# Summing the last MLP chunk's activations in three pieces of 128 tokens, one ahead of each tile

## The chip, the cores and the metric

The kernel runs on one core of one Trainium2 chip. The metric is device time in microseconds (us) for one execution. Before the change it is 2811.47 us, the median of three runs that lie between 2810.86 and 2814.71 us. All data are 32-bit floats.

## What is computed

The reference is one transformer block on a 48 x 48 grid of tokens with 768 channels, followed by a spectral layer on the same grid. Cut to what matters here:

```
x   = x + attention(layernorm(x)) @ proj_w + proj_b
xn2 = layernorm(x)
h   = gelu(xn2 @ mlp_w1 + mlp_b1)          # 2304 x 3072
x   = x + (h @ mlp_w2 + mlp_b2)            # 2304 x 768
x   = x + irfft2(soft-shrunk two-layer mix of rfft2(x))
```

The change lies at the end of the second product of the MLP, `h @ mlp_w2`, and just ahead of the spectral layer.

## The kernel before

**Staging.** The attention comes first, then the MLP, then the spectral layer. The result `x` stays in SBUF all the time, as 18 tiles of 128 tokens by 768 channels (`main`, also called `x1`). The MLP walks over three groups of 768 tokens (`p`), and within each over 12 chunks of 256 hidden features (`n`). One chunk makes its activations `h` (2 blocks of 128 features by 768 tokens) in the generator `hidden` and adds their share of the output in `added`, in three calls `i` = 0, 1, 2. Call `i` handles two tiles of 128 tokens at once, one from each half of the group's 768 tokens. "Tile" below means such a call.

**Seven products instead of eight.** Both matrix products are split into 2 x 2 blocks and computed with seven block products (a scheme of Strassen's kind). That needs sums of blocks beforehand. For the second product, `left` (lines 160 to 164) makes them from the activations on VectorE: four operations on 128 x 384 elements. With a11, a12, a21, a22 the four blocks of `h`, line 161 writes s1 = a21 + a22, line 162 writes s2 = s1 - a11, line 163 writes s4 = a12 - s2, and line 164 overwrites a21 with s3 = a11 - a21. Both inputs of each of them lie in SBUF. Line 162 waits for 161 by a semaphore, and 163 for 162; 164 waits for nothing.

**The seven products of a tile**, in `added` (lines 1403 to 1413), in their order on TensorE:

```
nc.tensor.matmul(bank[0], a11, b11, start=True, stop=True)   # p0: needs no sum
product(1, s2, t2, True, acc[i])     # p1: needs line 162
product(2, s3, t3, True, x22)        # p2: needs line 164
product(3, s1, t1, True, x22)        # p3
product(0, a12, b21, False, x11)     # p4
product(2, a22, t4, False, x21)      # p5
product(3, s4, b22, False, x12)      # p6
```

Each is followed by one VectorE operation that reads its PSUM bank and adds it to a tile in SBUF (line 1407 for p0, line 1401 for the others). In the last chunk of a group three more additions end the tile: line 1415 on VectorE (`x21 += acc`), lines 1416 and 1417 on GpSimd (called POOL in the profile; `x12 += acc`, `x22 += acc`). All three have both inputs in SBUF.

**Order of the work.** In this part of the kernel the order on every engine is the order in which the program is written (`manual_schedule`), and every engine takes its instructions strictly in that order. Within a group, the additions of chunk n - 1 are put between the stages of `hidden` of chunk n, so that TensorE has matrix products (line 1338) while `left` runs. After the last chunk (n = 11) there is no next chunk. In groups 0 and 1, transposes (`turned`) stand ahead of each of the three calls of `added`. In the last group (p = 2) nothing stands there: the three tiles follow directly on `left`. After them `rows_forward` (line 1419) begins the spectral layer with the products `zp` of line 1431.

**The rest of the chain.** The `zp` products are copied to SBUF (`zt`), stored to DRAM by the SP queue, and loaded back in another order as `zi`. Everything after that depends on them.

Of the kernel before, what the change touches and what calls it, by code (L numbers as in the profile page):

```python
# [19 lines left out]
P = 128  # L20
HW = 48
T = HW * HW
# [7 lines left out]
TB = 768  # L30
G = 384
# [15 lines left out]
def block_then_afno(  # L47
# [27 lines left out]
    nc = tc.nc  # L75
# [15 lines left out]
    def col(i):  # L91
        return vec[:, i : i + 1]
# [67 lines left out]
    def left(eng, a11, a12, a21, a22, s):  # L160
        eng.tensor_tensor(s[0], a21, a22, ALU.add)
        eng.tensor_tensor(s[1], s[0], a11, ALU.subtract)  # L162
        eng.tensor_tensor(s[2], a12, s[1], ALU.subtract)
        eng.tensor_tensor(a21, a11, a21, ALU.subtract)  # L164
# [16 lines left out]
    def parts_of_tokens(xt, xs, at=slice(None)):  # L181

        blocks = [xt[:, ds(3 * i, 3), ts(j, G)] for i, j in ((0, 0), (1, 0), (0, 1), (1, 1))]
        return [a[:, :, at] for a in (*blocks, *(xs[:, i] for i in range(3)))]
# [10 lines left out]
    with ExitStack() as flag_scope:  # L195
# [12 lines left out]
        with ExitStack() as att:  # L208
# [491 lines left out]
            with tc.manual_schedule(engines={mybir.EngineType.PE, mybir.EngineType.SP}):  # L700
# [161 lines left out]
                with tc.manual_schedule(  # L862
                    engines={mybir.EngineType.Activation, mybir.EngineType.DVE}
                ):
                    for pr in range(NC):
                        for c in range(T // G):
# [19 lines left out]
                            work = between(pr, c, acc)  # L886
# [166 lines left out]
        with tc.If(safe < 1):  # L1053
            with ExitStack() as att:
# [27 lines left out]
                for pr in range(NC):  # L1082
# [39 lines left out]
                    for sg in range(T // SG):  # L1122
# [20 lines left out]
                        for i in range(2):  # L1143
                            hp = psum.tile([P, G], F32, name="g_hp", tag="m")
                            for r in range(8):
                                h = sg * 16 + i * 8 + r
# [104 lines left out]
        with tc.tile_pool(name="ps_turn", bufs=4, space=PSUM) as psum_turn, tc.tile_pool(  # L1251
# [3 lines left out]
            for u in range(EARLY, PAIRS):  # L1255
# [5 lines left out]
                n = u - EARLY  # L1261
# [29 lines left out]
    with ExitStack() as mlp:  # L1291
# [10 lines left out]
        n_f = FF // FCH  # L1302
# [4 lines left out]
        def weights(p, n):  # L1307

            w = wpool.tile([P, NC, FCH], F32, name="w1")
            nc.sync.dma_start(  # L1310
                out=w, in_=mlp_w1[:, ts(n, FCH)].rearrange("(c p) f -> p c f", p=P)
            )
            ws = wpool.tile([P, 3, 3, P], F32, name="w1s")
            a11, a12, a21, a22 = (w[:, ds(3 * j, 3), ts(i, P)] for i in range(2) for j in range(2))
            left(nc.gpsimd, a11, a12, a21, a22, [ws[:, i] for i in range(3)])
            v = wpool.tile([P, 2, C], F32, name="w2")
            nc.sync.dma_start(
                out=v, in_=mlp_w2[ts(n, FCH), :].rearrange("(j p) c -> p j c", p=P)
            )
            vs = wpool.tile([P, 3, CH], F32, name="w2s")  # L1320
            right(
                nc.gpsimd, v[:, 0, :CH], v[:, 0, CH:], v[:, 1, :CH], v[:, 1, CH:],
                [vs[:, i] for i in range(3)],
            )
            ready_w[p, n] = a11, a12, a21, a22, ws, v, vs

        def hidden(p, n):

            a11, a12, a21, a22, ws, v, vs = ready_w.pop((p, n))
            h = hpool.tile([P, 2, TB], F32, name="hT")  # L1330
            hs = hpool.tile([P, 3, G], F32, name="hs", bufs=1)
            kept[p, n] = h, hs, v, vs

            bank = [psum.tile([P, G], F32, name=f"h{i}") for i in range(4)]

            def product(i, a, b, start):
                for c in range(3):
                    nc.tensor.matmul(  # L1338
                        bank[i], a[:, c, :], b[:, c, :],
                        start=(start and c == 0), stop=(c == 2), skip_group_check=not start,  # L1340
                    )

            def gelu(i, k, src):
                nc.scalar.activation(  # L1344
                    h[:, i, ts(k, G)], src, AF.Gelu, bias=col(V_B1 + 2 * n + i)
                )

            def summed(src, other, name, bufs=2):
                t = upool.tile([P, G], F32, name=name, bufs=bufs)
                nc.vector.tensor_tensor(t, src, other, ALU.add)  # L1350
                return t

            b11, b21, t3, b22, t1, t2, t4 = parts_of_tokens(xt, xs)
            s1, s2, s4 = (ws[:, i] for i in range(3))
            product(0, a11, b11, True)
            m1 = upool.tile([P, G], F32, name="m1")
            nc.scalar.copy(m1, bank[0])
            product(1, s2, t2, True)
            u = summed(bank[1], m1, "u")
            yield  # L1360
            product(2, a21, t3, True)
            u7 = summed(bank[2], u, "u7")
            product(3, s1, t1, True)
            gelu(1, 1, summed(bank[3], u7, "c", 3))
            yield
            product(0, a12, b21, False)
            gelu(0, 0, bank[0])
            product(2, a22, t4, False)
            gelu(1, 0, summed(bank[2], u, "c", 3))
            product(3, s4, b22, False)  # L1370
            gelu(0, 1, summed(bank[3], u, "c", 3))
            yield
            left(
                nc.vector, h[:, 0, :G], h[:, 1, :G], h[:, 0, G:], h[:, 1, G:],
                [hs[:, i] for i in range(3)],
            )
            yield

        acc = {}

        def added(p, n, i):

            h, hs, v, vs = kept[p, n]
            bank = [psum.tile([P, CH], F32, name=f"o{k}") for k in range(4)]
            if n == 0:
                acc[i] = upool.tile([P, CH], F32, name=f"acc{i}", bufs=1)
            a11, a12, s3, a22 = (
                h[:, f, ds(k * G + i * P, P)] for f, k in ((0, 0), (1, 0), (0, 1), (1, 1))
            )
            s1, s2, s4 = (hs[:, k, ts(i, P)] for k in range(3))  # L1390
            b11, t3, b21, b22 = (v[:, f, ts(k, CH)] for f in range(2) for k in range(2))
            t1, t2, t4 = (vs[:, k] for k in range(3))
            t = 2 * (p * 3) + i
            x11, x12, x21, x22 = (
                x1[:, t + 3 * j, ts(k, CH)] for j in range(2) for k in range(2)
            )

            def product(k, a, b, start, *into):
                nc.tensor.matmul(bank[k], a, b, start=start, stop=True, skip_group_check=not start)  # L1399
                for dst in into:  # L1400
                    nc.vector.tensor_tensor(dst, bank[k], dst, ALU.add)  # L1401

            nc.tensor.matmul(bank[0], a11, b11, start=True, stop=True)  # L1403
            if n == 0:
                nc.vector.tensor_copy(acc[i], bank[0])
            else:
                nc.vector.tensor_tensor(acc[i], bank[0], acc[i], ALU.add)
            product(1, s2, t2, True, acc[i])
            product(2, s3, t3, True, x22)
            product(3, s1, t1, True, x22)  # L1410
            product(0, a12, b21, False, x11)
            product(2, a22, t4, False, x21)
            product(3, s4, b22, False, x12)
            if n == n_f - 1:
                nc.vector.tensor_tensor(x21, x21, acc[i], ALU.add)
                nc.gpsimd.tensor_tensor(x12, x12, acc[i], ALU.add)
                nc.gpsimd.tensor_tensor(x22, x22, acc[i], ALU.add)
# [61 lines left out]
        def turned(piece):  # L1479

            for i in range(4 * piece, 4 * piece + 4):
                j, c = divmod(i, NC)
                tp = psum.tile([P, G], F32, name="tp2", tag=f"h{i % 4}")
                for k in range(3):
                    nc.tensor.transpose(tp[:, ts(k, P)], hats[3 * j + k][:, ts(c, P)], ident)  # L1485
                nc.scalar.activation(
                    xt[:, c, ts(j, G)], tp, AF.Identity, bias=col(V_LN2B + c), scale=col(V_LN2G + c)
                )
# [6 lines left out]
        for p in range(T // TB):  # L1495
            for n in range(n_f):
                if (p, n) == (0, 2):
                    nc.sync.dma_start(out=b2, in_=mlp_b2[0, :].partition_broadcast(P))
                    nc.sync.dma_start(out=rows_dft, in_=c_rows)
                work = hidden(p, n)  # L1500
                for i in range(3):
                    next(work)
                    if n:
                        added(p, n - 1, i)
                next(work)
                if n < n_f - 1 and (p == 0 or n):
                    weights(p, n + 1)
                if p < 2 and 3 <= n < 9:
                    measured(p + 1, n - 3)
                if p < 2 and n > 8:  # L1510
                    for i in range(2 * (n - 9), 2 * (n - 8)):
                        normalised(p + 1, i)
            for i in range(3):
                if p < 2:
                    turned(i)
                added(p, n_f - 1, i)
            if p < 2:
                sums_of_tokens(xt, xs)
                for n in range(2):
                    weights(p + 1, n)  # L1520
            rows_forward(p)
# [392 lines left out]
```

## Time and profile before

One execution was profiled. Its own time is 2813.01 us; the span from its first to its last instruction is 2811.2 us, so 1.8 us lie around the span.

| | before |
|---|---|
| median of 3 runs | 2811.47 us (2810.86 to 2814.71) |
| profiled execution | 2813.01 us, span 2811.2 us, mean granted TensorE clock 0.998 |
| TensorE matmuls (PE) | 2781.4 us busy, 99% of the span |
| TensorE weight loads (PEld) | 1715.4 us, 61% |
| VectorE (DVE) | 1700.5 us, 60% |
| ScalarE (ACT) | 916.2 us, 33% |
| GpSimd (POOL) | 662.7 us, 24% |
| three tiles of the last chunk, p0 of the first to first `zp` | 2545.21 to 2560.66 us in the span |

How to read the views that follow. A row of the timeline has the start of an instruction in us from the span's start, how long it took in us, engine, line, operation, what it writes and reads, and, in square brackets, how long the engine sat idle before it and what ended that. "x2" merges two instructions (every 32-bit product is two matmul records). In the view by groups, a row has the busy time in us and the mean ns of one instruction after the bar. In the view of windows, a row has a stretch, its length, and per engine the busy time; PEclk is the share of the TensorE clock that was granted.

### The profile page before, as it was taken

Reading aid. Unit: us, or ns where it says so; the run is one execution under the profiler, and the core shown is the slowest. Engines: PE = TensorE matmul, PEld = TensorE weight load, DVE = VectorE, ACT = ScalarE, POOL = GpSimd, SP = SyncE. Lnnn points to the kernel's source line nnn. Section 1 sums busy time; section 2 is a strip of 40 time slices with the busy share of each in tenths; the row PEclk is TensorE's granted clock in tenths of the full one; section 3 lists DMA queues with packets and bytes.
Section 4 is the critical chain, followed back from the end, with each engine's and each line's share of the span. In section 5 each row is a group of like instructions: output and inputs, shape, how many; then the busy total and the mean of one; then the engine's idle time right before and its main releaser. Section 6 shows DMA issues by size and latency. Waiting matters only on the chain. (4 is left out here: it accounts for less than half of the span.)

```text
span 2811.2 us, 40985 instructions
## 1 busy us (share of the span) xinstructions
PE 2781.4 (99%) x15765; PEld 1715.4 (61%) x15765; DVE 1700.5 (60%) x2505; ACT 916.2 (33%) x1456; POOL 662.7 (24%) x658
## 2 busy tenths in 40 slices
PE   8999999999999999999999999999999999999998
PEld 5555656666556566665555555555555555556887
DVE  4434246767676767676756566665666566566666
ACT  1101136656566666665501101121101201102332
POOL 2405110000000000000064332352232522322433
PEclk9999999999999999999999999999999999999999
DMA  5435376273663737546242112131121212123254
GB/s 177 162 107 168 99 157 120 50 137 63 106 127 65 132 63 124 99 77 102 90 156 79 58 61 67 45 102 57 45 67 62 96 45 68 45 65 113 63 161 146
DMA packets 216848, 269.08 MB, mean 96 GB/s; under 512 B 24600, under 2 KB 195472, under 8 KB 215108
## 3 DMA queue, kind: packets, MB, share of 16 engines
q1 hardware_dynamic: 215350, 265.25, 38.0%
q8 instruction: 127, 2.08, 0.3%
q10 hardware_dynamic: 1230, 0.92, 0.1%
q14 instruction: 77, 0.63, 0.1%
q0 software_dynamic: 64, 0.20, 0.0%
HBM read 150.25 MB, written 52.32 MB: 72 GB/s over the span
## 5 line engine op out<-in xcount | busy, mean ns | idle before, releaser
L736 ACT ACTIVATE main<-sp 128x768 f32<-128x768 f32 x648 | 516.1, 811 | 34.7 <-PE sp L726 19.3
L880 DVE TENSOR_TENSOR pairs<-pairs,main 128x1536 f32<-128x1536 f32 x252 | 443.0, 1758 | 27.2 <-DVE pairs L880 0.9
L726 PE MATMUL sp<-terms,select 64*128 64x384 f32 x1296 | 412.0, 629 | 0.0
L1401 DVE TENSOR_TENSOR main<-o,main 128x384 f32<-128x384 f32 x540 | 299.3, 557 | 43.1 <-PE o L1399 0.5
L1338 PE MATMUL h<-shared,w 128*128 128x384 f32 x864 | 296.6, 486 | 0.7 <-POOL w2s L167 0.7
L717 PE MATMUL sp<-shared 64*128 64x384 f32 x1296 | 265.2, 485 | 1.6 <-ACT row_hi L241 1.0
L717 PE MATMUL sp<-qT,kT 64*128 64x384 f32 x1296 | 264.1, 484 | 0.0
L1338 PEld LDWEIGHTS h<-shared,w 128*128 128x128 f32 x864 | 163.9, 190 | 116.2 <-POOL w2s L167 1.3
L782 POOL TENSOR_TENSOR inverse<-inverse,rden 24x32 f32<-24x32 f32 x36 | 14.9, 414 | 924.9 <-DVE sums L781 924.9
L1338 PE MATMUL h<-shared,w1s 128*128 128x384 f32 x648 | 226.7, 486 | 0.0
L749 PE MATMUL op<-main,shared 128*64 128x384 f32 x1296 | 217.4, 488 | 0.0
L749 PE MATMUL op<-main,v 128*64 128x384 f32 x1296 | 216.4, 488 | 0.0
L1344 ACT ACTIVATE hT<-c,vec 128x384 f32<-128x384 f32 x108 | 66.4, 615 | 457.6 <-DVE c L1350 457.5
L880 DVE TENSOR_TENSOR pairs<-main 128x1536 f32<-128x1536 f32 x36 | 63.3, 1758 | 245.8 <-ACT main L736 245.8
L1350 DVE TENSOR_TENSOR c<-h,u 128x384 f32<-128x384 f32 x108 | 60.2, 557 | 218.5 <-PE h L1338 218.5
L726 PEld LDWEIGHTS sp<-terms,select 64*128 64x128 f32 x1296 | 125.3, 186 | 83.7
L1399 PE MATMUL o<-w2s,hs 128*128 128x384 f32 x432 | 175.0, 487 | 1.2 <-DVE hs L162 1.2
L1399 PE MATMUL o<-w,hT 128*128 128x384 f32 x432 | 175.1, 487 | 0.8 <-DVE hT L164 0.5
L1338 PEld LDWEIGHTS h<-shared,w1s 128*128 128x128 f32 x648 | 123.1, 190 | 85.8
L167 POOL TENSOR_TENSOR w2s<-w 128x384 f32<-128x384 f32 x36 | 36.0, 999 | 576.8 <-DMA w<-in_mlp_w_dram 429.4
L749 PEld LDWEIGHTS op<-main,v 128*64 128x64 f32 x1296 | 96.8, 137 | 92.7 <-issue 67.7
L749 PEld LDWEIGHTS op<-main,shared 128*64 128x64 f32 x1296 | 96.4, 137 | 89.4 <-issue 64.4
(222 smaller groups left out, 4176.9 us busy)
## 6 DMA issues: line engine op xcount, KB each, us to landing
w<-in_mlp_w_dram SPq DMA_DIRECT2D x72, 768.0 KB
terms<-col_parts SPq DMA_DIRECT2D x432, 72.0 KB
terms<-row_hi SPq DMA_DIRECT2D x216, 72.0 KB
terms<-row_lo SPq DMA_DIRECT2D x216, 72.0 KB
main<-in_qkv_w_dram SPq DMA_DIRECT2D x36, 384.0 KB
z<-zt SPq DMA_DIRECT2D x48, 192.0 KB
x<-in_x_blocks_dram SPq DMA_DIRECT2D x18, 384.0 KB
q_d<-o SPq DMA_DIRECT2D x36, 192.0 KB
```

The costliest lines, as they stand in the source:

```text
L167: eng.tensor_tensor(t[0], b12, b11, ALU.subtract)
L717: nc.tensor.matmul(sp[:, j, :G], kT[at, ts(kt, P)], qT[at, ts(c, G)], start=first, stop=not first,)
L726: nc.tensor.matmul(sp[:, j, :G], select[at, a % 2], ready[pr, c][at, a // 2, b], start=first, stop=not first,)
L736: nc.scalar.activation(p, sp[:, :, :G], AF.Exp, scale=HD**-0.5)
L749: nc.tensor.matmul(op[ts(j, 64)], v[:, kt, ts(j, 64)], exps[:, kt, j, :], start=(kt == 0), stop=(kt == NT - 1),)
L782: nc.gpsimd.tensor_tensor(inverse[:ND], inverse[:ND], rden, ALU.add)
L880: nc.vector.tensor_tensor(pairs, so_far, exps[:, ds(kt - 1, 2)], ALU.add)
L1338: nc.tensor.matmul(bank[i], a[:, c, :], b[:, c, :], start=(start and c == 0), stop=(c == 2), skip_group_check=not start,)
L1344: nc.scalar.activation(h[:, i, ts(k, G)], src, AF.Gelu, bias=col(V_B1 + 2 * n + i))
L1350: nc.vector.tensor_tensor(t, src, other, ALU.add)
L1399: nc.tensor.matmul(bank[k], a, b, start=start, stop=True, skip_group_check=not start)
L1401: nc.vector.tensor_tensor(dst, bank[k], dst, ALU.add)
```

## The change

Only in the last chunk of the last group, `left` is no longer made in one piece of 384 columns but in three pieces of 128 columns (one tile's tokens each). The first piece stands where the whole stood; the second and the third stand ahead of `added` of tile 1 and tile 2. In all other chunks the order and the sizes are as before.

```diff
@@ hidden
             yield
-            left(
-                nc.vector, h[:, 0, :G], h[:, 1, :G], h[:, 0, G:], h[:, 1, G:],
-                [hs[:, i] for i in range(3)],
-            )
-            yield
+            pieces = [slice(0, G)]
+            if (p, n) == (T // TB - 1, n_f - 1):
+                pieces = [slice(i * P, i * P + P) for i in range(3)]
+            for at in pieces:
+                left(
+                    nc.vector, h[:, 0, :G][:, at], h[:, 1, :G][:, at],
+                    h[:, 0, G:][:, at], h[:, 1, G:][:, at], [hs[:, i, at] for i in range(3)],
+                )
+                yield
@@ block_then_afno, after the loop over chunks
             for i in range(3):
                 if p < 2:
                     turned(i)
+                elif i:
+                    next(work)
                 added(p, n_f - 1, i)
```

On VectorE, four instructions on 128 x 384 become twelve on 128 x 128: four ahead of tile 0's additions, four between tile 0's line 1415 and tile 1's line 1407, and four at the same place ahead of tile 2. The order on TensorE, ScalarE, GpSimd and in the DMA queues stays as it was. On TensorE, p1 of tiles 1 and 2 now waits for VectorE (line 162 of its piece), and so does p2 (line 164 of its piece).

## Prediction

> **What bounds the kernel now.** I read the page first: TensorE's matmuls fill the span, VectorE has a third of it free.
>
> ```profile
> PE 2781.4 (99%) x15765; PEld 1715.4 (61%) x15765; DVE 1700.5 (60%) x2505; ACT 916.2 (33%) x1456; POOL 662.7 (24%) x658
> ```
>
> So a change gains only where TensorE sits idle. The list of waits in the stretch 2540 to 2562 us shows TensorE waiting for `left` once: 1.2 us for line 162 and 0.2 us for line 164. Then the timeline of the last chunk's three tiles (all engines), where I followed p0 to p6 of tile 0 and the end of its VectorE and GpSimd work:
>
> ```profile
> 2545.21 0.81 PE L1403 MATMUL o<-w,hT 128*128 128x384 f32 x2
> 2545.89 0.55 DVE L161 TENSOR_TENSOR hs<-hT 128x384 f32<-128x384 f32 x1
> 2546.47 0.56 DVE L162 TENSOR_TENSOR hs<-hs,hT 128x384 f32<-128x384 f32 x1
> ...
> 2547.17 0.88 PE L1399 MATMUL o<-w2s,hs 128*128 128x384 f32 x2 [1.15 <-DVE hs L162]
> ...
> 2548.23 0.88 PE L1399 MATMUL o<-w,hT 128*128 128x384 f32 x2 [0.18 <-DVE hT L164]
> ...
> 2550.89 0.81 PE L1399 MATMUL o<-w,hs 128*128 128x384 f32 x2
> ...
> 2552.21 0.55 DVE L1415 TENSOR_TENSOR main<-main,acc 128x384 f32<-128x384 f32 x1
> 2552.37 1.24 POOL L1416 TENSOR_TENSOR main<-main,acc 128x384 f32<-128x384 f32 x1 [26.26 <-DVE main L1401]
> ...
> 2553.57 0.99 POOL L1417 TENSOR_TENSOR main<-main,acc 128x384 f32<-128x384 f32 x1
> ```
>
> The reader is to see three things. p1 starts at 2547.17, 0.14 us after line 162 ended (2546.47 + 0.56); p2 starts at 2548.23, 0.14 us after line 164 ended. Undisturbed products follow each other every 0.645 us (2548.95, 2549.60, 2550.24, 2550.89). And VectorE ends a tile late: line 1415 starts 1.32 us after p6 started, when TensorE is already past p0 and due to start p1 of the next tile.
>
> **What is gained: tile 0.** From p0 at 2545.21, p3 was due 3 x 0.645 later, at 2547.145; it started at 2548.95. So `left` costs 1.80 us today. In the new kernel its first piece has 128 columns. No row has that width on two SBUF inputs; by form, a VectorE operation on two tensors takes 254 ns for 96 columns (line 1630), 351 for 192 (line 1656) and 554 for 384 (line 1656). Between the first two, 128 columns take about 0.285 us. The shortest VectorE row I found (209 ns, line 1462) and the 0.555 us of the full width are the bounds; I take 0.285, which lies between its two nearest widths. Line 161 starts at 2545.89 as before, since VectorE is busy with the tile ahead until then; 162 starts 0.03 after 161 ends (as in the rows) and ends at 2546.49; p1 starts at 2546.63, where it was due at 2545.855: 0.78 lost, and 0.07 more because the product after a stall took 0.72 instead of 0.645 (2548.23 to 2548.95). Line 164 ends at 2547.01 (it starts 0.08 before 163's end, as in the rows), ahead of p2's turn at 2547.345. Loss 0.85 instead of 1.80: **0.95 us gained**.
>
> **What is added: tiles 1 and 2.** Here there is no wait before; the sums are long made. Now VectorE makes piece 1 after tile 0's line 1415, and p1 of tile 1 waits for it. Call X the start of the previous tile's p6 (2550.89 above). p1 is due at X + 1.29. Line 1415 starts at X + 1.32, and the instruction behind it started 0.46 later in the old order (2552.67), so line 161 can start at X + 1.78, end of 162 at X + 2.38, p1 at X + 2.52: 1.23 + 0.07 = 1.30 us lost, even if nothing disturbs VectorE. On VectorE, all of the tile's seven additions are queued behind the piece, but they wait for TensorE's products anyway.
>
> Something does disturb it. GpSimd runs lines 1416 and 1417 of the tile before from X + 1.48 to X + 3.67, and they have two SBUF inputs as the four lines of `left` have. What that means is seen in the first chunk of the MLP (timeline from 1560 us), where GpSimd's sums of weights meet `left`:
>
> ```profile
> 1561.59 0.56 DVE L163 TENSOR_TENSOR hs<-hT,hs 128x384 f32<-128x384 f32 x1
> 1561.66 1.34 POOL L161 TENSOR_TENSOR w1s<-w 128x384 f32<-128x384 f32 x1 [5.23 <-DMA w<-in_mlp_w_dram]
> 1562.07 1.35 DVE L164 TENSOR_TENSOR hT<-hT 128x384 f32<-128x384 f32 x1
> ```
>
> Line 164 took 1.35 us instead of its usual 0.55, and GpSimd's 1.34 instead of 1.00. They took turns: GpSimd had to let 163 end, then 164 had to let GpSimd end (at 1563.00) and ended 0.42 us after it. Line 1416's own 1.24 us beside line 1415 are the same thing. So in tile 1: 1416 has waited since X + 1.48 and goes as soon as 1415 is through, ends at X + 2.72 (as today, 2553.61), and line 161 ends 0.15 after it (0.42 less 0.27 for 256 columns fewer), at X + 2.87. Line 1417, at its place since X + 2.68, goes next, before line 162, which must first see 161's semaphore at X + 2.90; 1417 needs 1.00 and ends at X + 3.72. Line 162 ends 0.15 later, at X + 3.87, and **p1 starts at X + 4.01**. Lost: 4.01 - 1.29 + 0.07 = 2.79 us. Lines 163 and 164 then have the way free; 164 ends at X + 4.39, p2 could start at X + 4.53 and is due at X + 4.73, no further stall. Tile 2 repeats this: 5.58 us in all. If VectorE went first instead, I get 161 undisturbed but 162 behind 1416 and 163 behind 1417, p2 late, and about 2.5 us a tile: the turn hardly matters.
>
> Nothing covers it: TensorE takes its products in order and `zp` (line 1431) follows 0.74 us behind the last p6. No DMA and no other engine's order is moved; all after `zp` depends on it and shifts along. Sum so far: 5.58 - 0.95 = **+4.63 us**.
>
> **The clock.** TensorE idles from the end of p0 (X + 0.645 + 0.81) to X + 4.01: 2.55 us, twice. In the trace, changes of the granted clock fall on a grid of 3.41 us. I asked the windows view for the stretches ahead of the two drops; the second, near the end:
>
> ```profile
> 2792.70:2796.11 3.41, 1.36 (x18) 0.97 (x16) 1.24 (x4) 0.00 (x0) 0.00 (x0) 1.00 0.68 224
> 2796.11:2799.52 3.41, 3.41 (x25) 3.15 (x23) 1.07 (x3) 0.00 (x0) 0.00 (x0) 0.50 0.68 229
> ```
>
> After a stretch with TensorE busy for 1.36 of 3.41 us (one gap of 2.05 us, waiting for `zl`) the next stretch ran at half clock. After 1.15 busy us (1464.91 on; a gap of 3.76 us) it was two stretches. After 2.50 busy us (2543.52 on, the stall of tile 0 today) the clock stayed at 1.00. A gap of 2.55 us leaves only 0.86 us of busy time if it lies within one stretch. It has at least 2.05 us in one stretch for 1.86 of the 3.41 us of possible positions, 55%; if a smaller share is enough (anything down to the 0.92 us that did no harm), up to 100%. I take 75% for each gap. A drop costs 3.41 us at half rate, all of it in products where the stretch begins behind the gap (1.7 us lost), less where up to 0.5 us of the gap lies in it (1.45): 1.6. Two drops: **+3.2 us**.
>
> The Trainium skill, on its page "TensorE: Matmul & The Clock Gate", section "Why this matters for your kernels", asks only that TensorE's idle gaps stay under about 3 us. By that rule the gaps of 2.55 us would cost no clock and the sum would stay at +4.6; this case's row with a gap of 2.05 us and half a clock behind it speaks against it, and I go by the row.
>
> **The sum.** -0.95 + 5.58 + 3.2 = +7.8 us: the profiled execution would go from 2813.01 (span 2811.2 and 1.8 around it) to 2820.8. That execution lay 1.54 above the median of the runs; from the median 2811.47, **2819.3 us**. What a measurement of this kernel can tell from no change is about 0.2%, or 5.6 us.
>
> **The rivals.**
> 1. *Lock without drops, or with one.* The position of the stretches is chance: one drop gives 4.63 + 1.6 = +6.2 (2817.7), none +4.6 (2816.1), not measurably slower. For it: no stretch with a busy time between 1.36 and 2.50 us was seen at full clock, and the 1.36 were narrower matmuls (64 columns).
> 2. *VectorE and GpSimd don't collide.* If a 128-column operation slips between GpSimd's reads, only 2 x 1.30 - 0.95 = +1.65 us remains, and gaps of 1.06 us (X + 1.455 to X + 2.52) that trip nothing: 2813.1. Against it: line 164's 1.35 us and line 1416's 1.24.
> 3. *The other side: it does what it says.* If pieces 1 and 2 were ready before p1's turn, only tile 0's gain stays: -0.95, 2810.5, not slower. It decides itself at one point: line 162 of a piece must end by X + 1.15 (p1's turn less 0.14). VectorE would have to make the piece in a hole ahead of p6's addition; but it takes its instructions in order, and line 1415, ahead of the piece, starts only at X + 1.32.
>
> **How the numbers follow.** Forecast, collision with two drops, 33%; one drop 27%; none 15%; no collision 15%; the pieces cost nothing 4%; more than any of these, 6%. The range: the low end takes in no collision, 2813.0. For the high end I take the full-width price for a 128-column operation: 0.27 more for each of lines 161 and 162, three times 0.54 = +1.6, with two drops 2820.9, and some 0.6 for the spread of the runs: 2821.5. At the cheapest price, 0.21, each tile saves 0.15, so 2818.8. Slower by over 0.2%: 33 + 27 + 6, less 4 for cases that fall just short, 62%. Within 0.2%: 36%. Faster by over 0.2%: 2%, for nothing here gives 5.6 us.
>
> **What would show it.** In the changed kernel's timeline: p1 of tile 0 at about 1.4 us after its p0 instead of 1.96; p1 of tiles 1 and 2 with idle time of about 2.5 us before them, ended by line 162; lines 161 and 162 of pieces 2 and 3 with rows of 0.9 to 1.1 us instead of 0.29, in step with lines 1416 and 1417; first `zp` 4.6 us later, or up to 7.8 with half clock in the windows behind the gaps. Wrong if the gaps are 1.1 us (no collision), if there are none (rival 3), or if the clock in the windows stays 1.00.

## The result, and the profile after

The changed kernel takes **2819.67 us**, the median of 11 runs (2814.45 to 2823.86). The kernel before, in 11 runs beside it, takes 2812.39 us (2809.76 to 2814.84). The ratio is 1.0026, with a 95% interval from 1.0018 to 1.0033; the medians are 7.28 us apart. So the change makes the kernel slower by a quarter of a per cent. The prediction was 2819.3 us.

The profiled execution of the changed kernel took 2823.72 us, nearly the longest of the eleven, with a span of 2821.9 us and a mean clock of 0.996 (before: 2813.01, 2811.2, 0.998). The engine line of its page has nearly the same busy times as before; of VectorE it shows the eight instructions that were added:

```profile
PE 2785.7 (99%) x15765; PEld 1717.0 (61%) x15765; DVE 1703.4 (60%) x2513; ACT 916.8 (32%) x1456; POOL 663.5 (24%) x658
```

TensorE's list of waits in the stretch 2545 to 2569 us, the last chunk, names one wait (total, times, longest). Before it was 1.2 us for line 162 and 0.2 us for line 164:

```profile
PE o L1403 <- DVE hs L162: 5.6, 3, 2.5
```

The timeline (all engines) of tile 0 and of the border to tile 1 shows where these 5.6 us come from. The file is a few lines longer, so that line 1401 of before is now 1405, 1403 is 1407, 1399 is 1403, 1415 to 1417 are 1419 to 1421:

```profile
2546.52 0.81 PE L1407 MATMUL o<-w,hT 128*128 128x384 f32 x2
2547.20 0.28 DVE L161 TENSOR_TENSOR hs<-hT 128x128 f32<-128x128 f32 x1
2547.51 0.29 DVE L162 TENSOR_TENSOR hs<-hs,hT 128x128 f32<-128x128 f32 x1
...
2547.95 0.88 PE L1403 MATMUL o<-w2s,hs 128*128 128x384 f32 x2 [0.62 <-DVE hs L162]
...
2551.25 0.81 PE L1403 MATMUL o<-w,hs 128*128 128x384 f32 x2
...
2552.57 0.55 DVE L1419 TENSOR_TENSOR main<-main,acc 128x384 f32<-128x384 f32 x1
2552.73 1.24 POOL L1420 TENSOR_TENSOR main<-main,acc 128x384 f32<-128x384 f32 x1 [25.26 <-DVE main L1405]
2553.04 1.08 DVE L161 TENSOR_TENSOR hs<-hT 128x128 f32<-128x128 f32 x1
2553.93 1.03 POOL L1421 TENSOR_TENSOR main<-main,acc 128x384 f32<-128x384 f32 x1
2554.15 0.96 DVE L162 TENSOR_TENSOR hs<-hs,hT 128x128 f32<-128x128 f32 x1
...
2555.17 1.50 PE L1403 MATMUL o<-w2s,hs 128*128 128x384 f32 x2 [2.47 <-DVE hs L162]
```

The reader is to see two things. In tile 0, alone on VectorE, lines 161 and 162 take 0.28 and 0.29 us, and p1 follows p0 after 1.43 us instead of 1.96. At the border to tile 1 the same two instructions take 1.08 and 0.96 us, in step with GpSimd's lines 1420 and 1421, and TensorE stands still for 2.47 us. The border to tile 2 repeats it within a hundredth (1.08, 0.97, a gap of 2.47).

The view by windows gives the clock behind these two gaps. A row has a stretch, its length, the busy time of PE, PEld, DVE, ACT and POOL with the number of instructions, the granted clock, the DMA share and GB/s:

```profile
2551.94:2555.35 3.41, 0.94 (x4) 0.33 (x3) 3.25 (x6) 0.00 (x0) 2.23 (x2) 1.00 0.00 0
2555.36:2558.77 3.41, 3.41 (x6) 1.86 (x6) 1.87 (x5) 0.00 (x0) 0.00 (x0) 0.50 0.00 0
2562.18:2565.59 3.41, 1.47 (x5) 0.94 (x6) 3.24 (x6) 0.00 (x0) 1.73 (x2) 1.00 0.00 0
2565.59:2569.01 3.42, 3.42 (x15) 1.72 (x15) 3.07 (x7) 0.00 (x0) 0.08 (x1) 1.00 0.00 0
```

The first gap (2552.70 to 2555.17) lies wholly in one stretch, and the next one ran at half clock. The second, as long, was cut by a border of stretches: the one that holds most of it still had 1.47 us of work, and the clock stayed.

From p0 of tile 0 to the first `zp`, the stretch in which the change acts, went 21.66 us instead of 15.45: **+6.21 us**. From the first `zp` to the end of the span went 253.74 instead of 250.54, 3.2 us more. That the prediction had not foreseen, and a second profile of the same kernel doesn't have it: see below.

### The profile page after: what moved, and what is told of

Its sections match the earlier page's. It is cut to its first block, busy times and chain, and to the rows that moved or that the text cites. A ratio compares the mean times of both kernels' runs of the same rounds, so it can differ in the third digit from the quotient of the medians.

```text
span 2821.9 us, 40992 instructions
## 1 busy us (share of the span) xinstructions
PE 2785.7 (99%) x15765; PEld 1717.0 (61%) x15765; DVE 1703.4 (60%) x2513; ACT 916.8 (32%) x1456; POOL 663.5 (24%) x658
## 3 DMA queue, kind: packets, MB, share of 16 engines
q8 instruction: 127, 2.08, 0.3%
```

## The experiments

**Theories.** *Turns and clock* (the prediction's): a piece for tiles 1 and 2 starts behind line 1419; its lines 161 and 162 take turns with GpSimd's 1420 and 1421, and the gaps this opens halve the clock, or don't, by where they fall. *No turns*: VectorE's instructions are long for another reason, and only the late place of the piece matters. *No clock*: the gaps alone make the loss; half clock is chance and there before the change too. *Later*: the loss lies behind `zp`, in the spectral layer.

In all that follows "local" is the time from p0 of tile 0 to the first `zp` in the one profiled execution (before: 15.45 us), and "after `zp`" is the time from there to the end of the span (before: 250.54 us).

### The changed kernel once more

The kernel is the changed one, not a line different: how much do its runs scatter, and does the clock fall otherwise?

> The changed kernel once more, to be timed beside the others and for a second profile. Both theories: +7 us against the kernel before, with a gap of 2.47 us in tiles 1 and 2. Theory of the clock: half clock behind one or both gaps, depending on how they lie to the grid of 3.41 us; with both, first zp 7.8 us later than before counted from tile 0's p0, with one 6.2, with none 4.5.

Measured: 2819.65 us (2814.86 to 2823.10, 11 runs); beside it before 2813.67; ratio 1.0020 (1.0011 to 1.0029). The local time is 23.31 us, +7.86, and the windows show why it is longer than in the first profile. They are the stretches ahead of and behind the two gaps:

```profile
2549.03:2552.44 3.41, 1.02 (x4) 0.27 (x2) 3.29 (x5) 0.00 (x0) 2.23 (x2) 1.00 0.00 0
2552.44:2555.86 3.42, 3.35 (x5) 1.85 (x6) 1.92 (x6) 0.00 (x0) 0.00 (x0) 0.50 0.00 0
2559.27:2562.68 3.41, 1.27 (x4) 0.86 (x5) 3.24 (x7) 0.00 (x0) 1.93 (x2) 1.00 0.00 0
2562.68:2566.10 3.42, 3.42 (x6) 1.69 (x5) 1.83 (x4) 0.00 (x0) 0.00 (x0) 0.50 0.00 0
```

Here both gaps halve the clock. Same kernel, same gaps, one stretch at half clock in one execution, two in the other.

### GpSimd's additions after the last tile

Lines 1420 and 1421 of the last group's last chunk are kept back until all three tiles are done, so that GpSimd is idle while the pieces are made. (From the changed kernel.)

```diff
         acc = {}
+        late = []
@@ added
-                nc.gpsimd.tensor_tensor(x12, x12, acc[i], ALU.add)
-                nc.gpsimd.tensor_tensor(x22, x22, acc[i], ALU.add)
+                late.append((x12, x22, acc[i]))
+                if p < 2 or i == 2:
+                    tiles = late[-1:] + late[:-1]
+                    for k in range(2):
+                        for both in tiles:
+                            nc.gpsimd.tensor_tensor(both[k], both[k], both[2], ALU.add)
+                    late.clear()
```

> The changed kernel, but GpSimd's six additions that end the three tiles of the last chunk stand behind tile 2's additions (tile 2's first), so that GpSimd is idle while VectorE makes pieces 2 and 3. Theory (GpSimd's reads and the pieces take turns, and the long gaps drop the clock): the four operations of a piece take 0.28 us each, p1 of tiles 1 and 2 starts 2.5 us after the previous p6 instead of 3.92, the gaps are about 1.06 us, no half clock behind them; 2 x 1.30 - 0.94 = +1.7 us against the kernel before. Rival (the pieces are slow by themselves, or TensorE's wait has another cause): gaps stay near 2.5 us and the time stays at +7.

Measured: 2812.85 us (2811.81 to 2814.99, 11 runs) beside 2813.67; ratio 0.9999 (0.9990 to 1.0008). The timeline at the border to tile 1:

```profile
2549.88 0.81 PE L1404 MATMUL o<-w,hs 128*128 128x384 f32 x2
...
2551.66 0.28 DVE L161 TENSOR_TENSOR hs<-hT 128x128 f32<-128x128 f32 x1
2551.98 0.29 DVE L162 TENSOR_TENSOR hs<-hs,hT 128x128 f32<-128x128 f32 x1
...
2552.33 0.91 PE L1404 MATMUL o<-w2s,hs 128*128 128x384 f32 x2 [1.00 <-DVE hs L162]
```

With GpSimd out of the way the two instructions take 0.28 and 0.29 us, as in tile 0. The gap is 1.00 us instead of 2.47, p1 comes 2.45 us after p6 instead of 3.92, no stretch of the last chunk lost its clock, and the local loss is +1.58 us. That rules out *no turns*. What is left, 2.45 - 1.29 and 0.10 for a slower product behind the stall, 1.26 us a tile, is the late place alone.

### Spare products in the gaps

Behind p0 of tiles 1 and 2, TensorE makes three products (or one) whose results nobody reads, into free PSUM banks, so that it isn't idle while the piece is made. Gap and turns stay, the idle time goes. (From the changed kernel; the second has `range(1)`.)

```diff
             nc.tensor.matmul(bank[0], a11, b11, start=True, stop=True)
+            if (p, n) == (T // TB - 1, n_f - 1) and i:
+                for k in range(3):
+                    spare = psum.tile([P, G], F32, name="spare", tag=f"h{k}")
+                    nc.tensor.matmul(spare, a11, b11, start=True, stop=True)
```

> The changed kernel, with three spare products into unused PSUM banks between p0 and p1 of tiles 1 and 2 (their results are not used), which keep TensorE busy for 1.94 us of each gap and delay nothing. Theory: p1 still starts 3.92 us after the previous p6, the stall is as long, but the clock stays at 1.00 behind both gaps; -0.94 + 2 x 2.70 = +4.5 us against the kernel before, 2 to 3 us less than the changed kernel. Rival (the clock costs nothing that counts, and what goes beyond 4.5 us is scatter of the last transfers): the same time as the changed kernel run beside it.

> As e2_spare_products, with one spare product (0.65 us) instead of three in each gap, so 1.83 us of each gap stay idle. Theory of the clock (a stretch of the 3.41 us grid with less than about 1.45 us busy halves the clock of the next): at least 1.58 us busy in any stretch, never a drop, p0 to zp 19.98 us as with three. Rival (any gap near 2 us trips it, as a gap of 2.05 us did at the end of the kernel): a drop behind one or both gaps, 21.6 or more. On the 5 us that e2 lost after zp: if they are scatter of the transfers, +4.5 us against the kernel before; if the spare products themselves cause it, +9 again.

Measured with one spare product: 2817.15 us (2815.39 to 2819.73, 11 runs) beside 2813.21; ratio 1.0016 (1.0007 to 1.0025). By the whole time alone this can't be told from the changed kernel's 1.0020 to 1.0026, whose intervals overlap with it; the trace tells more. Its windows, the stretches that hold most of the two gaps:

```profile
2550.02:2553.43 3.41, 2.18 (x7) 1.39 (x8) 3.21 (x7) 0.00 (x0) 1.02 (x2) 1.00 0.00 0
...
2556.84:2560.25 3.41, 1.75 (x6) 1.09 (x7) 3.24 (x7) 0.00 (x0) 1.46 (x2) 1.00 0.00 0
```

The stretches are fuller, 2.18 and 1.75 us instead of 0.94 to 1.47, and the clock was 1.00 in those behind them too. p1 comes 3.92 us after p6 as before, so the wait itself has its full price, and the local loss is +4.52 us. This is the price of the change without the clock; against +6.21 with one stretch at half clock and +7.86 with two, a stretch costs 1.69 and 1.67 us.

With three spare products the local loss is the same, +4.53 us (gaps of 0.54 us, no half clock in them), yet the whole took 2823.45 us (2822.38 to 2824.52, 5 runs) beside 2813.67; ratio 1.0037 (1.0023 to 1.0051). That is a miss of the expectation. Some 5 us were lost after `zp`: 255.07 us instead of 250.54. The next three kernels are about that.

### Where do three spare products lose 5 us after `zp`?

SP's list of waits in the stretch behind `zp` (2565 to 2585 us) of the kernel with three spare products says that the loads of `zi` waited 3.8 us for the stores of `zt`:

```profile
SPq L1287 <- DMA z<-zt: 3.8, 1, 3.8
```

In the kernel before, the same wait is 2.3 us in three pieces, in the changed kernel 1.6. First suspect: the PSUM banks that the spare products write (`h0` to `h2`; `zp` itself writes `o0` to `o3`), or the scatter of one kernel's transfers. So all three went to a single other bank:

```diff
-                    spare = psum.tile([P, G], F32, name="spare", tag=f"h{k}")
+                    spare = psum.tile([P, G], F32, name="spare", tag="h3")
```

> e2_spare_products with the three spare products in another PSUM bank, as a second build of the same work: p0 to zp 19.98 us and no half clock by the theory. What is open is the end: if the transfers behind zp scatter by themselves, its time is near +4.5 us; if the spare products cause what e2 lost there, near +9 again.

Measured: 2822.56 us (2821.90 to 2825.16, 5 runs) beside 2813.21; ratio 1.0038 (1.0024 to 1.0051); local +4.53, after `zp` 255.74 us, the wait of the `zi` loads 3.6 us. The loss came back: the choice of banks isn't it, nor the scatter of one kernel.

Second suspect: the number of instructions on TensorE, which shifts the place at which its code is fetched from memory (the page of the kernel before has a DMA queue of kind "instruction" with 127 packets and 2.08 MB, 16 KB each), so that such a fetch could meet the stores. The spare products put 24 instructions ahead of `zp` (six products, each two matmuls and two weight loads). In one kernel as many, and in the other 232 more, were put elsewhere, far ahead, at the last group's first chunk: tiny products with one column.

```diff
+                if (p, n) == (T // TB - 1, 0):
+                    for k in range(6):
+                        pad = psum.tile([P, G], F32, name="pad", tag="h0")
+                        nc.tensor.matmul(pad[:, :1], ones, ones[:, :1], start=True, stop=True)
                 work = hidden(p, n)
```

The kernel before with 6 of them:

> The kernel before with six spare products of one column at the start of the last group (24 more TensorE instructions, results not used), as many more as the six spare products of e2 and e8 brought. What is open is why those two lost 5 us after zp. Theory: TensorE's code is fetched by the DMA engines in pieces of 16 KB; 24 more instructions move a fetch to 8.3 to 9.3 us after the first zp, among the stores of z that the first load of zi waits for (that wait 3.6 to 3.8 us instead of 1.4 to 2.3). Then this kernel loses there too: zp to the end 2 to 5 us longer, +3 to +6 us against the kernel before. Rival (the spare products in the gaps themselves, or the state they leave): only the six products' own time, +0.8 us or less, the wait for the stores 1.4 to 2.3 us.

The kernel with three spare products and 58 of them:

> e2_spare_products with 58 spare products of one column at the start of the last group (232 TensorE instructions, which with the 24 of the spare products make 256, 16 KB of code, so that fetches fall where they fall without both). Theory of the code fetches: the first load of zi waits for the stores 1.4 to 2.3 us again instead of 3.8, zp to the end falls from 255 to about 250 to 252 us; p0 to zp stays 19.98. The 58 products cost time of their own where they stand (5 to 12 us by estimate), so the whole is no measure here. Rival: 3.6 us and 255 us stay.

Measured: with 6 of them ahead, the kernel before takes 2818.34 us (2815.68 to 2820.30, 11 runs) beside 2812.47; ratio 1.0016 (1.0007 to 1.0026). Its local time is 15.45 us as before, but the padding itself cost some 4 of the 5.87 us: 2.6 us of its own and a stretch of 3.4 us at half clock behind it (2235.4 to 2238.8), which misses 1.7. The wait of the `zi` loads is 1.5 us. The time after `zp` is 253.05 us, 2.5 more than before, but all of it in the last load `zl` (7.65 us instead of 5.17), which begins 229.95 us after the first `zp`, as before (229.91); with the spare products it begins at 232.90 and 232.48. So the loss was not reproduced. With 58 more beside the spare products, the longest such wait went down to 1.4 us and the time after `zp` back to 250.70 us. The whole took 2856.18 us (2855.34 to 2856.91, 4 runs; ratio 1.0157, 1.0141 to 1.0172), since 35.6 us around the padding were spent at a mean clock of 0.54, far more than expected of so small products. So the spare products don't bring the 5 us by themselves: what stands far ahead on TensorE can take them away. That the fetch of code does it was only argued, and the traces speak against its simple form: a 16 KB packet of the instruction queue starts 9.30 and 8.26 us after the first `zp` in the two kernels that lose, and at 8.99 us, between them, in the kernel with 6 paddings, which doesn't. **It stays open**, with one profile of each kernel. For the change it doesn't matter: the changed kernel has no instruction more on TensorE than before, and its wait is 1.6 us.

### All of it on GpSimd

Lines 161 to 164 of the last chunk on GpSimd, in one piece, from the kernel before: can the sums be made without VectorE?

```diff
-                nc.vector, h[:, 0, :G], h[:, 1, :G], h[:, 0, G:], h[:, 1, G:],
+                nc.gpsimd if (p, n) == (T // TB - 1, n_f - 1) else nc.vector, h[:, 0, :G], h[:, 1, :G], h[:, 0, G:], h[:, 1, G:],
```

> The kernel before, with the four sums of the last chunk (one piece of 384 columns) on GpSimd, which is idle there. GpSimd needs 1.0 us each, and can start when the last activation is there, 4 us before VectorE could: line 162 would end about 1.8 us and line 164 about 0.3 us ahead of p1's and p2's turn. Theory (the 1.80 us stall of tile 0 is only VectorE being late): no wait of TensorE in tile 0, -1.8 us against the kernel before. Rival (GpSimd's sums collide with VectorE's operations on two SBUF inputs and come late): a stall of 1 us or more stays, 0 to -0.8 us.

Measured: 2817.08 us (2814.38 to 2819.91, 11 runs) beside 2813.67; ratio 1.0011 (1.0002 to 1.0020), local +1.46. GpSimd was free 19 us early and yet began late, as the timeline shows with p1:

```profile
2545.99 1.00 POOL L161 TENSOR_TENSOR hs<-hT 128x384 f32<-128x384 f32 x1 [19.43 <-PE o L1399]
...
2548.12 0.91 PE L1399 MATMUL o<-w2s,hs 128*128 128x384 f32 x2 [1.62 <-POOL hs L162]
```

What released it was line 1399: TensorE's last read of the previous chunk's `hs`, which has a single buffer. p1 waited 1.62 us, and p2 another 1.11 us for line 164. The whole lost 3.4 us, more than this: its runs miss 7.95 us of clock on average, those of before beside it 5.33, so that half clock may be the rest; the one profile, the fastest of the 11 runs, shows none there. VectorE doesn't feel this wait, since it is busy with that chunk's additions until then. So the same once more with a buffer of its own, one of the buffers for sums of weights, which no later chunk needs (added to the edit above):

```diff
-            hs = hpool.tile([P, 3, G], F32, name="hs", bufs=1)
+            if (p, n) == (T // TB - 1, n_f - 1):
+                hs = wpool.tile([P, 3, 3, P], F32, name="w1s").rearrange("p k c t -> p k (c t)")
+            else:
+                hs = hpool.tile([P, 3, G], F32, name="hs", bufs=1)
```

> As e3_left_on_gpsimd (one piece of 384 columns on GpSimd, in the kernel before), but the three sums go to a buffer of their own, since in e3 GpSimd had to wait for TensorE to have read the sums of chunk 10 in the single buffer. Theory (the first stall is only VectorE being late, and e3 only showed the buffer): GpSimd starts about 0.1 us after the last activation, line 162 ends about 2.2 us and line 164 about 4.2 us after it, p1 and p2 of tile 0 run at their turn, p0 of tile 0 to the first zp falls from 15.45 to 13.65 us, -1.8 us against the kernel before. Rival (GpSimd collides with VectorE's operation on two SBUF inputs that stands there and comes late): 14.5 us or more.

Measured: the timeline shows GpSimd beginning as soon as the activations are there, and p1 and p2 following p0 without idle time, 0.65 and 0.64 us apart:

```profile
2540.57 0.99 POOL L161 TENSOR_TENSOR w1s<-hT 128x384 f32<-128x384 f32 x1 [15.97 <-ACT hT L1347]
...
2543.76 0.81 PE L1406 MATMUL o<-w,hT 128*128 128x384 f32 x2
...
2544.41 0.81 PE L1402 MATMUL o<-w2s,w1s 128*128 128x384 f32 x2
...
2545.05 0.81 PE L1402 MATMUL o<-w,hT 128*128 128x384 f32 x2
```

The local time is 13.64 us, 1.81 less than before: the whole of the 1.80 us that `left` costs there. The whole took 2811.73 us (2809.01 to 2817.11, 11 runs) beside 2813.21; ratio 0.9998, and the interval (0.9989 to 1.0007) has no change in it. The gain is seen in the trace and is too small to be seen in the time.

### All pieces ahead of tile 0

Two pieces, 128 and 256 columns, both ahead of tile 0's additions: the early p1 without the late pieces. (From the changed kernel.)

```diff
-                pieces = [slice(i * P, i * P + P) for i in range(3)]
+                pieces = [slice(0, P), slice(P, G)]
@@
-                elif i:
+                elif i == 0:
                     next(work)
```

> The changed kernel with the second and the third piece as one (256 columns) directly behind the first, ahead of tile 0's additions on VectorE. Theory: p1 of tile 0 starts as in the changed kernel (1.43 us after p0), no wait in tiles 1 and 2, but tile 0's additions come 1.55 us later, so p4 waits for bank 0 about 0.6 us and p5 for bank 2 about as much; -0.94 + 1.1 to 1.2, p0 to zp 15.4 to 15.8, within 0.5 us of the kernel before. Rival (VectorE has the room): -0.9 us.

Measured: 2813.18 us (2810.60 to 2817.73, 11 runs) beside 2813.21; ratio 1.0001 (0.9992 to 1.0010); local +0.13 us. The first piece is as early as in the changed kernel, and then the second stands ahead of the additions that free TensorE's banks:

```profile
2548.14 0.42 DVE L161 TENSOR_TENSOR hs<-hT 128x256 f32<-128x256 f32 x1
...
2549.73 0.55 DVE L1411 TENSOR_TENSOR acc<-o,acc 128x384 f32<-128x384 f32 x1
...
2550.34 0.91 PE L1403 MATMUL o<-w,hT 128*128 128x384 f32 x2 [0.32 <-DVE acc L1411]
```

p4 now waits 0.32 us for VectorE's addition, and p5 another 0.21 us for the next. The two pieces together take 2.72 us on VectorE (one piece before: 2.20), the tile's additions come only after them, and TensorE catches up with these: what the first piece gains, p4 and p5 give back.

### The runs side by side

| kernel | median us | beside it, before | ratio (95%) | local, against 15.45 | half-clock stretches in it | after `zp` |
|---|---|---|---|---|---|---|
| changed | 2819.67 | 2812.39 | 1.0026 (1.0018 to 1.0033) | +6.21 | 1 | 253.74 |
| changed, again | 2819.65 | 2813.67 | 1.0020 (1.0011 to 1.0029) | +7.86 | 2 | 249.67 |
| one spare product | 2817.15 | 2813.21 | 1.0016 (1.0007 to 1.0025) | +4.52 | 0 | 251.73 |
| GpSimd's additions last | 2812.85 | 2813.67 | 0.9999 (0.9990 to 1.0008) | +1.58 | 0 | 249.85 |
| two pieces ahead | 2813.18 | 2813.21 | 1.0001 (0.9992 to 1.0010) | +0.13 | 0 | 253.95 |
| on GpSimd, own buffer | 2811.73 | 2813.21 | 0.9998 (0.9989 to 1.0007) | -1.81 | 0 | 249.98 |

**What the mean clocks say.** Each run comes with its mean clock, in thousandths; a thousandth missing is 2.8 us of clock, and a stretch of 3.41 us at half clock misses 1.7. Over the 22 runs of the changed kernel 7.05 us are missing on average, over 69 runs of the kernel before 4.69 us. The difference, 2.4 us (my standard error from the scatter of the runs: 0.7), is some 1.4 stretches more in each run. This is a rough measure, as it counts half clock wherever it falls, also where no product runs, as at the end of the span. But the 11 runs with one spare product in each gap, with the same waits, miss 4.61 us, as many as before. Runs with equal clock can be compared too: at 0.997 the medians are 2820.51 us (10 runs) and 2815.70 us (12), 4.8 apart; at 0.998 they are 2818.59 (4) and 2813.76 (31), 4.8 apart; at 0.999 they are 2814.93 (5) and 2811.97 (17), 3.0 apart. That brackets the 4.52 of the kernel whose clock was kept up. So both parts are there in the runs that no profile shows: about 4.5 us of waiting and about 2.4 us of clock. *No clock* falls with this and with the kernel of one spare product; *later* falls with the time after `zp`, which is 3.2 us longer in one profile of the changed kernel and 0.9 us shorter in the other.

## Why the prediction was right

**Tile 0's gain.** Predicted 0.95 us, with 0.285 us for an operation of 128 columns. The rows are 0.28 and 0.29; p0 to p3 took 2.80 us instead of 3.74, 0.94 us gained.

**The place of the piece.** Predicted: line 161 cannot start before X + 1.78, X being the start of the previous tile's p6. It started at 2553.04, with X = 2551.25 that is X + 1.79. The kernel with GpSimd's additions last shows this part alone: p1 at X + 2.45 (predicted 2.52).

**The turns with GpSimd.** Predicted ends: 161 at X + 2.87, the second GpSimd addition at X + 3.72, 162 at X + 3.87. Measured: X + 2.87, X + 3.71, X + 3.86. That it is GpSimd, and not something else, is shown by the kernel that takes its two additions away. p1 came at X + 3.92 and not X + 4.01, as it started 0.06 us after line 162's end, not 0.14. The product behind it took 0.74 us instead of 0.645, so a tile loses 3.92 - 1.29 + 0.10 = 2.73 us (predicted 2.79), the two 5.46, and with tile 0's gain the sum is **+4.52 us** (predicted +4.63; +4.52 measured where the clock was kept). The Trainium skill, "SBUF — State Buffer", section "Who interferes with whom", calls the port pair that VectorE shares with GpSimd an exclusive lock; the rows agree (1.08 us for an operation that takes 0.28 alone). They show the order beside it: line 162 ended only after GpSimd's second addition. The prediction's reason for this order, that line 162 must first wait for line 161's semaphore while GpSimd's addition stands ready, fits the rows to 0.01 us, but no run takes that wait away, so the reason is not shown by itself.

**The clock.** Predicted 1.6 us for a stretch, measured 1.67 to 1.69. Predicted 75% for a gap to cost one, 1.5 in a run; two profiles show 1 and 2, the mean clocks 1.4. The likeliest case of the prediction, two drops, was given only a third, and one of the two profiles has it; the other has rival 1's case of one drop. With the measured terms the mean is 4.5 + 1.4 x 1.67 = 6.8 us; the two comparisons have 7.28 and 5.98. That 2819.3 and 2819.67 lie only 0.4 us apart is in part luck: the forecast added 7.8 us, a case that not every run has, to a median of three runs, 2811.47, which lay 0.9 us below the median of the 11 runs beside the changed kernel. The rule of the skill that the prediction weighed, "TensorE: Matmul & The Clock Gate", section "Why this matters for your kernels", would have left gaps below about 3 us free. The gaps of 2.47 us weren't; the row of the kernel before had it right.

**What the prediction gave no term for.** The 3.2 us after `zp` in the profiled execution. TensorE's timeline from `zp` on is the same as before until 235 us later, when it waits for the last `zl`. The chain of waits of the changed kernel, near its end:

```profile
2798.12 7.09 DMA zl<-z
...
2805.35 10.32 PE rps L1725 x88
```

and of the kernel before:

```profile
2790.57 5.17 DMA zl<-z
...
2795.87 9.06 PE rps L1719 x88
```

The load took 7.09 us instead of 5.17, TensorE idled 4.0 us instead of 2.0, and half clock lasted twice as long behind it. This doesn't come with the change each time: in its second profile the load took 5.31 us, no half clock came behind it, and the time after `zp` was 249.67, less than before's; in the other kernels the load took between 5.15 and 8.40 us, in no order that follows the edits. Why it varies stays open. Had the profile been compared with the profile of before alone, the change would have been charged 10.7 us instead of 6 to 7.

**The rivals.** Rival 2, no collision (+1.65), is what the kernel with GpSimd's additions last came to, +1.58: the price was right, the condition didn't hold. Rival 3, all pieces ready in time, decided itself where the prediction put the point: line 162 had to end by X + 1.15 and ended at X + 3.86.

## What to carry to other kernels

Cutting an operation into pieces makes the first one earlier and the others later: price each piece by the end of what stands ahead of it on its engine, and look at what the neighbour engine is doing at that very moment, since a VectorE operation of 0.28 us became 1.08 beside a GpSimd addition of two SBUF inputs. A wait of 2.5 us on TensorE has a second price, half clock for the next 3.4 us, that depends on where the gap falls and so comes as a chance. Where an engine has 16 us of idle time, as GpSimd here, moving the whole operation there takes the wait away, once the buffer that it writes is free early enough; the 1.8 us gained here are seen in the trace alone.

## What the runs showed of the hardware

- **Where the clock drops.** For the products of the last chunk: stretches of 3.41 us in which TensorE was busy for 0.94, 1.02 and 1.27 us were followed by half clock; those with 1.47, 1.75 and 2.18 weren't. For smaller products the limit isn't always the same: behind 1.78 us of the `fp` products (96 columns), in the spectral layer of the kernel with two pieces ahead, the clock went to 0.50 for two stretches; behind 1.79 us of the `rps` products (192 columns), near the end of the kernel with three spare products, it stayed, and behind 1.44 us it fell.
- **One-column products don't hold the clock up.** With 58 of them, the records show TensorE busy for 32.26 of 35.6 us, at a mean clock of 0.54.
- **The scatter of the kernel before goes mostly with the clock.** Its 69 runs have medians of 2810.41 us at clock 1.000 (9 runs), 2811.97 at 0.999 (17), 2813.76 at 0.998 (31) and 2815.70 at 0.997 (12). Besides the gaps of the change, the paddings and the end of the span, the profiles of all kernels show half clock near 1470 us (in 11 of 12), behind the wait for `zl` (in 7 of 12) and, in one, early in the spectral layer; where it falls differs from run to run.
